# Graph layer on one Trainium2 core: small constant and counting work of the front, moved between VectorE and GpSimd

## The chip, the cores and the metric

The kernel runs on one core of one Trainium2 chip. The metric is the device time of one execution in microseconds. The times before are 1309.93, 1305.32 and 1305.66 us: a median of 1305.66.

The engines are called as the profile calls them: PE (TensorE; PEld is its weight load), DVE (VectorE), ACT (ScalarE), POOL (GpSimd) and SP (SyncE, which only issues DMAs here).

## The reference

```python
h = jnp.maximum(_layernorm(x, axis=-1), 0.0)          # x: 12500 x 128
xs = h[src]                                            # 200000 edges
for i in range(4):                                     # edge types
    mask = (edge_type_4 == i)[:, None]
    msgs = msgs + jnp.where(mask, xs @ W[i] + b[i], 0.0)
return x + jax.ops.segment_sum(msgs, dst, num_segments=12500)
```

The edges are sorted by dst, and dst is drawn as 12500 u², so that the first nodes have very many edges and the last ones few.

## The kernel before, in words

All 200000 edges are taken in chunks of 128. The first C0 = 576 chunks, whose nodes have many edges, are handled densely: for each "slot" (a unit of one to three nodes) PE counts, by a product of two one-hot matrices, how many edges come from each node and of each type, and the counts are then multiplied with the whole table of normalised rows. The other 987 chunks are handled by gathering: GpSimd fetches the 128 rows of a chunk from the table with an indirect DMA, PE sums them by node and type with a one-hot matrix, and DVE adds the results into a ring of sums.

Before this can run at full speed there is the **front**, in which these things go on side by side:

- The table. 33 units of three rows of nodes per partition are loaded from x (`load_span`, on SP's queue). DVE takes statistics (`look`, L519), L523 to L528 make a variance of them, ACT takes the root with `eps` as bias (L531), DVE the reciprocal and the shift (L534, L535), and ACT writes the normalised rows h (L540). PE, ACT and DVE split h into three 16-bit parts (L566 to L582), and SP stores these into htab (L584).
- The rows of x for the first 48 gathered chunks. GpSimd fetches them from x itself (`gather_raw`, L606, 48 indirect DMAs), since the table is not there yet; from the fourth pair on, the gathers are held back behind the statistics of certain units. DVE takes their statistics too, and ACT normalises them (also L540, tile hx).
- The slots (`make_slots`). d1 holds the node that each slot begins with (L926; for further blocks of a node with many edges it is copied by GpSimd, L931). `first_chunk` compares it with the first node of each dense chunk (L937), PE counts the chunks below it (L946), and L950 writes the number qa of the chunk in which the slot's first node lies, for UNITS = 866 units in two pieces of 433. L957 adds each unit's capacity in chunks, `caps`, which gives nth. L961 writes qa of the further blocks, qa of the unit plus the number k of the block, for the slots 866 to 1050. `pick_out` then compares qa and nth with the chunks' numbers (L937 again, the tiles sel), PE picks the edge data with L986, and L994 to L998 put it into `packed`; pieces of 433 come first, then those of the further blocks, in pieces of 185 and below. `unpack` (L1010 on) makes of it what the counting uses.
- Small constants: iotas on GpSimd, their conversions on DVE, memsets.
- `span`, the number of places (nodes) that each gathered chunk may reach: 128 x 8, begun at 10 with a memset and raised in eight steps (L324 to L333), each of a comparison and an addition. It goes into the key of each edge (L362) and into a check of the limits (L370, later L392 and L396).

The order in which each engine meets these instructions is not written by hand in the front: a planner lays it out from the order of the text, the dependencies and its own idea of the costs. It becomes a hand-written order for PE, DVE and ACT only at line 1596 (`manual_schedule`), behind the front. GpSimd's and SP's queues are the planner's throughout. Every engine takes its queue strictly in order. After the front, `pace` distributes the dense work over the groups of gathered chunks.

`eps` is not a plain constant before the change: L489 multiplies an element of srcT (the first transposed source indices) by zero, and L490 adds EPS / UP² to that. So eps, and with it every root, waits for srcT and for two instructions on DVE.

`marks` is a list of instructions of which the last ten hold back some later gathers (L629). The mark of L962 stands at the head of the list, before those of `pick_out` and of `unpack`, of which there are twelve alone; it is not among the last ten.

Of the kernel before, what the change touches and what calls it, by code (L numbers as in the profile page):

```python
# [35 lines left out]
F32 = mybir.dt.float32  # L36
BF16 = mybir.dt.bfloat16
F16 = mybir.dt.float16
# [6 lines left out]
ALU = mybir.AluOpType  # L45
# [5 lines left out]
P = 128  # L51
EPS = 1e-5
# [5 lines left out]
C0 = 576  # L58
# [21 lines left out]
UP = 4096.0  # L80
# [9 lines left out]
def kernel(  # L90
# [10 lines left out]
    nc = tc.nc  # L101
    N, D = x.shape
    E = src.shape[0]
    NT, _, DO = w.shape
# [36 lines left out]
    segs = []  # L141
    for d0, d1, size in ((TWOS, THREES, 2), (HEAVY, ONES, 3), (AFTER, TWOS, 3), (THREES, ND, 3), (ONES, AFTER, 1), (0, HEAVY, 1)):
        segs.append((sum(n for _, n, *_ in segs), (d1 - d0) // size, d0, size, [chunks_of(d, size) for d in range(d0, d1, size)]))
    UNITS = sum(n for _, n, *_ in segs)
    blocks = {}
    NS = 0
    for k, s in (
# [4 lines left out]
        n = sum(c > k for c in segs[s][4])  # L152
# [16 lines left out]
    def window_of(c):  # L169

        m = min((c - C0) // G, FULL)
        end = (C0 + (m + 1) * G if m < FULL else T) * P / E
        a_node = E * ((end**2 + 1 / N) ** 0.5 - end)
        return next((n for n in range(8, WIN, 2) if (n - 1) * a_node > P + 5 * P**0.5), WIN)
# [107 lines left out]
    const = ctx.enter_context(tc.tile_pool(name="const", bufs=1))  # L282
# [6 lines left out]
    srcT = const.tile([P, TURN, P], I32, name="srcT")  # L289
# [31 lines left out]
    row_i = prep.tile([P, BM], I32, name="row_i")  # L321
    nc.gpsimd.iota(row_i, pattern=[[P, BM]], base=0, channel_multiplier=1)
    rowf = const.tile([P, BM], F32, name="rowf")
    nc.vector.tensor_copy(rowf, row_i)  # L324

    span = const.tile([P, BM], F32, name="span")
    more = prep.tile([P, BM], F32, name="more")
    nc.vector.memset(span, float(window_of(C0)))
    for m in range(G, TM, G):
        wider = window_of(C0 + m) - window_of(C0 + m - G)  # L330
        if wider:
            nc.vector.tensor_scalar(more, rowf, m - 0.5, float(wider), ALU.is_gt, ALU.mult)
            nc.vector.tensor_add(span, span, more)  # L333
    QB = max(2, DENSE)

    def prep_edges(m0, m1, prep, QB):
# [148 lines left out]
    nc.vector.memset(ones_b, 1.0)  # L485
    eps = const.tile([P, 1], F32, name="eps")

    zero = const.tile([P, 1], F32, name="zero")
    nc.vector.tensor_single_scalar(zero, srcT[:, 0, 0:1], 0.0, op=ALU.mult)  # L489
    nc.vector.tensor_single_scalar(eps, zero, EPS / UP**2, op=ALU.add)  # L490
    pick = prep.tile([P, NT, N3], BF16, name="pick")
    nc.vector.memset(pick, 0.0)
    for t in range(NT):
# [98 lines left out]
    marks = []  # L592
# [315 lines left out]
    def make_slots(dix):  # L908

        def pieces(a, z, of=512):  # L910
            n = -(-(z - a) // of)
            return [(a + (z - a) * i // n, a + (z - a) * (i + 1) // n) for i in range(n)]

        d1 = dix.tile([P, NS], F16, name="d1")
        qa = dix.tile([P, NS], F16, name="qa")
        nth = dix.tile([P, UNITS], F16, name="nth")
        packed = dix.tile([P, NS], F32, name="packed")
        at_nodes = {}
        for (k, s), (c0, n) in blocks.items():
# [30 lines left out]
            nc.vector.tensor_scalar(qa[:, a:z], pq[:, : z - a], -1.0, 0.0, ALU.add, ALU.max)  # L950

        yield from pipelined(first_chunk(a, z) for a, z in pieces(0, UNITS))
        for u0, n, _, _, caps in segs:
            i = 0
            while i < n:
                m = sum(c == caps[i] for c in caps)
                nc.vector.tensor_single_scalar(nth[:, u0 + i : u0 + i + m], qa[:, u0 + i : u0 + i + m], float(caps[i]), op=ALU.add)  # L957
                i += m
        for (k, s), (c0, n) in blocks.items():
            if k:  # L960
                last = nc.vector.tensor_single_scalar(qa[:, c0 : c0 + n], qa[:, segs[s][0] : segs[s][0] + n], float(k), op=ALU.add)  # L961
        marks.append(last.ins)  # L962
        yield True

        def runs(a, z):
# [98 lines left out]
        for s, (_, n, d0, size, _) in enumerate(segs):  # L1064
            for a, z in pieces(0, n * size):
                pn = x_ps.tile([P, 512], F32, name="pt")
                todo = [(at_nodes[k, r], m * size) for (k, r), (_, m) in blocks.items() if r == s and m * size > a]
                for i, (w0, m) in enumerate(todo):
                    m = min(m, z)
# [337 lines left out]
    building = ExitStack()  # L1407
    dix = building.enter_context(tc.tile_pool(name="dix", bufs=1, side="right"))
    to_slots = make_slots(dix)
    work = None  # L1410
    dense_out = False
# [83 lines left out]
    for gi, us in enumerate(group_of):  # L1495
# [9 lines left out]
        for i, u in enumerate(us):  # L1505
# [7 lines left out]
            last = None  # L1513
            for l in more_looks[:each]:
                last = l()
# [194 lines left out]
    with tc.If(rv > 0):  # L1710
        with tc.tile_pool(name="slow", bufs=1) as slow, tc.tile_pool(name="slow_ps", bufs=1, space=PSUM) as slow_ps:
            zero = slow.tile([P, DO], F32, name="zero")
# [120 lines left out]
```

## Time and profile before

| | |
|---|---|
| median of 3 runs | 1305.66 us |
| lowest, highest | 1305.32, 1309.93 us |
| the profiled execution, its time | 1311.28 us |
| its span, first to last instruction | 1309.6 us |
| busy: PE, DVE, ACT, POOL | 1227.2, 1072.4, 1064.0, 954.0 us |
| mean granted TensorE clock | 0.962 |

Rows of the profile read thus. A row of the timeline has the start and the length in microseconds, the engine, the line of the kernel, the operation, the tile written and the tiles read, the shape, and xN for N instructions merged into one row; in brackets stands the idle time of the engine just before, and who ended it. A row of the groups has the shapes, the count, the busy time in microseconds, the mean duration in nanoseconds, and the idle time before. A row of the windows has the busy time of each engine in a stretch of time. The chain of waits is followed back from the last instruction to whatever released each step.

### The profile page before, as it was taken

The page shows a single profiled execution, that of the slowest core. Times are in us where ns is not written, and L with a number is a line of the kernel's source. Part 1 is how long each engine was busy: PE and PEld are TensorE (multiplying, and loading weights), DVE is VectorE, ACT ScalarE, POOL GpSimd, SP SyncE. Part 2 cuts the span into 40 slices and gives each one's busy share as a digit, 9 for nine tenths or more (in the row PEclk, how much of TensorE's full clock was granted, in tenths as well). Part 3 has the DMA queues.
Part 4 walks back from the last instruction along what each step waited for, and adds up shares of the span by engine and source line. Part 5 has one row for each costly group of instructions (what it writes and reads, how often), then busy time and mean ns, then how long its engine had stood idle before and what let it go on. Part 6 is the DMA issues. An engine that isn't in the chain of part 4 may idle for free.

```text
span 1309.6 us, 30266 instructions
## 1 busy us (share of the span) xinstructions
PE 1227.2 (94%) x9190; PEld 878.9 (67%) x9190; DVE 1072.4 (82%) x5214; ACT 1064.0 (81%) x1814; POOL 954.0 (73%) x1028
## 2 busy tenths in 40 slices
PE   4887898799999999999999999999999999999996
PEld 1345655577777777777777776777777777777775
DVE  8996487897898987989888887879888797978454
ACT  6795644498988989899898988889888898888881
POOL 6727577777777777777777777777777777777772
PEclk9895689799999999999999999999999999999998
DMA  8644289888888888888787877878788788787982
GB/s 252 215 172 145 60 253 335 287 281 254 268 270 253 258 273 259 260 256 275 245 268 243 286 236 254 259 231 276 235 269 250 242 268 252 254 246 242 290 277 83
DMA packets 184229, 321.75 MB, mean 246 GB/s; under 512 B 30100, under 2 KB 82253, under 8 KB 184061
## 3 DMA queue, kind: packets, MB, share of 16 engines
q1 hardware_dynamic: 132701, 214.63, 50.2%
q0 software_dynamic: 46608, 95.52, 25.6%
q10 hardware_dynamic: 4752, 9.64, 1.9%
q8 instruction: 72, 1.18, 0.4%
q14 instruction: 96, 0.79, 0.2%
HBM read 293.99 MB, written 25.67 MB: 244 GB/s over the span
## 4 chain that ended last, share of the span: by engine, by line
PE 81%; ACT 8%; DVE 6%; DMA 2%; issue 2%; SPq 0%; DVEq 0%; ACTq 0%
PE pa L1244 22%; PE pa L1252 22%; PE pt L1138 11%; PE py L701 8%; PE ps L675 7%; ACT dec L1206 2%; PE pt L1297 2%; DMA dtab<-dec 1%; PE pa L1274 1%; DVE ring L764 1%; ACT h L540 1%; PE ps L733 1%; DVE o L1103 1%; PE pt L986 1%; DVE o L1113 1%
## 5 line engine op out<-in xcount | busy, mean ns | idle before, releaser
L622 POOL DMA_INDIRECT hm<-htab,srcT x939 | 900.8, 959 | 311.6 <-issue 194.1
L1206 ACT ACTIVATE dec<-counts 128x1116 fp32r<-128x1116 uint8 (+1 forms) x594 | 676.1, 1162 | 10.2 <-PE pa L1244 7.6
L1103 DVE TENSOR_SCALAR o<-iota_w,hkT 128x392 bf16<-128x392 f16 x1051 | 429.3, 408 | 114.8 <-PE pt L1138 113.3
L1244 PE MATMUL pa<-dec,hs 128*128 128x372 f32 x1764 | 389.9, 355 | 0.0
L1252 PE MATMUL pa<-counts,hs 128*128 128x372 fp8e4 x1764 | 342.5, 327 | 7.8 <-ACT sd L1290 7.8
L1146 ACT CAST counts<-pt 128x396 int32<-128x396 f32 x587 | 292.1, 523 | 39.5 <-PE pt L1138 15.2
L1244 PEld LDWEIGHTS pa<-dec,hs 128*128 128x128 f32 x1764 | 302.3, 188 | 15.6 <-issue 0.3
L1138 PE MATMUL pt<-o,o 128*128 128x396 bf16 x1051 | 280.1, 338 | 12.9 <-DVE o L1113 11.3
L1252 PEld LDWEIGHTS <-hs 128*128 128x128 f16 x1764 | 165.3, 97 | 121.3 <-issue 12.3
L1113 DVE TENSOR_SCALAR o<-iota_b,loT,byT 128x128 bf16<-128x128 bf16 x746 | 245.5, 329 | 0.0
L764 DVE TENSOR_TENSOR ring<-ring,py 128x14 f32 (+6 forms) x912 | 158.4, 174 | 58.0 <-issue 13.0
L665 ACT ACTIVATE sb<-ps 128x224 f32<-128x224 f32 (+7 forms) x235 | 102.6, 437 | 104.7 <-PE py L701 87.5
L675 PEld LDWEIGHTS <-hm 128*128 128x128 f16 x2817 | 142.9, 99 | 66.4 <-issue 13.3
L675 PE MATMUL ps<-oh,hm 128*128 128x56 bf16 (+7 forms) x2817 | 174.0, 198 | 1.6 <-DMA hm<-htab,srcT 1.6
L640 DVE TENSOR_SCALAR oh<-iota_b,keyT 128x56 bf16<-128x56 bf16 (+7 forms) x939 | 161.0, 261 | 6.8 <-PE ps L675 6.8
L701 PE MATMUL py<-sb,wsb 128*128 128x224 f32 (+6 forms) x456 | 122.3, 412 | 0.0
L1138 PEld LDWEIGHTS <-o 128*128 128x128 bf16 x1051 | 82.3, 98 | 55.5 <-DVE o L1113 16.0
L701 PEld LDWEIGHTS py<-sb,wsb 128*128 128x128 f32 x456 | 83.3, 193 | 26.4 <-ACT counts L1146 4.3
L1113 DVE TENSOR_SCALAR o<-iota_b,loT 128x128 bf16<-128x128 bf16 x305 | 83.0, 272 | 0.0
L606 POOL DMA_INDIRECT hx<-in_x_dram,srcT x48 | 46.8, 974 | 22.6 <-issue 9.3
L1274 PE MATMUL pa<-counts,hs 128*128 128x348 fp8e4 x294 | 53.0, 325 | 0.4 <-DMA hs<-htab 0.4
L696 ACT CAST cnt<-pt 128x224 bf16<-128x224 f32 (+10 forms) x61 | 25.7, 421 | 26.1 <-PE pt L692 24.5
(253 smaller groups left out, 789.8 us busy)
## 6 DMA issues: line engine op xcount, KB each, us to landing
hs<-dtab SPq DMA_DIRECT2D x576, 288.0 KB
hm<-htab,srcT POOLq DMA_INDIRECT x939
htab<-h SPq DMA_DIRECT2D x32, 288.0 KB
hs<-htab SPq DMA_DIRECT2D x32, 288.0 KB
dtab<-dec ACTq DMA_DIRECT2D x32, 288.0 KB
xo<-in_x_dram SPq DMA_DIRECT2D x23, 256.0 KB
out_dram<-xo SPq DMA_DIRECT2D x23, 256.0 KB
hm<-in_x_dram SPq DMA_DIRECT2D x18, 192.0 KB
```

The lines of the kernel that those rows point to most:

```text
L622: one = nc.gpsimd.indirect_dma_start(out=hm[:, (i - h0) * D3 : (i - h0 + 1) * D3], out_offset=None, in_=htab, in_offset=bass.IndirectOffse ...
L640: nc.vector.tensor_scalar(oh[:, i, :], iota_b[:, :K], keyf[:, at : at + 1], None, ALU.is_equal)
L675: nc.tensor.matmul(ps[:, i - i0, :], rows(i, c), oh[:, i, :], start=(c == 0), stop=(c == 2))
L701: nc.tensor.matmul(py[:, :g, :], wsb[:, t, :], sb[0][:, :g, t, :], start=False, stop=(t == NT - 1))
L764: nc.vector.tensor_tensor(to, to, of(i), ALU.add)
L1103: one = nc.vector.tensor_scalar(o2[:, k, :NB].rearrange("p (r n) -> p r n", r=ROWS), iota_w, hkT[:, s : s + 1], None, ALU.is_equal)
L1113: one = nc.vector.tensor_scalar(o1[:, k], iota_b, loT[:, s : s + 1], by, ALU.is_equal, ALU.mult)
L1138: one = nc.tensor.matmul(pb, o1, o2, start=first, stop=last)
L1146: lambda i=i, pb=pb: nc.scalar.copy(counts[:, :, i * NT : (i + 1) * NT], pb.rearrange("p (b t) -> p b t", t=NT))
L1206: nc.scalar.activation(decoded[n][:, : j1 - j0, :nv].rearrange("p j (m v) -> p j m v", m=3), by_digit[:, j0:j1, : nu * NT * 4].rearrange(" ...
L1244: nc.tensor.matmul(to.rearrange("p (m v) -> p m v", m=3), row.bitcast(F32R)[:, D // 2 :], decoded[j // DS][:, j % DS, :nv].rearrange("p (m ...
L1252: nc.tensor.matmul(to.rearrange("p (m v) -> p m v", m=3), row[:, :D], counts[:, j, : nu * NT * 4].rearrange("p (v m) -> p m v", m=4)[:, :3 ...
```

## The change

Three places of the front are changed, and nothing behind it.

```diff
     rowf = const.tile([P, BM], F32, name="rowf")
-    nc.vector.tensor_copy(rowf, row_i)
+    nc.gpsimd.tensor_copy(rowf, row_i)
...
-    nc.vector.memset(span, float(window_of(C0)))
+    nc.gpsimd.memset(span, float(window_of(C0)))
     for m in range(G, TM, G):
         wider = window_of(C0 + m) - window_of(C0 + m - G)
         if wider:
-            nc.vector.tensor_scalar(more, rowf, m - 0.5, float(wider), ALU.is_gt, ALU.mult)
-            nc.vector.tensor_add(span, span, more)
+            nc.gpsimd.tensor_scalar(more, rowf, m - 0.5, float(wider), ALU.is_gt, ALU.mult)
+            nc.gpsimd.tensor_tensor(span, span, more, ALU.add)
...
-    zero = const.tile([P, 1], F32, name="zero")
-    nc.vector.tensor_single_scalar(zero, srcT[:, 0, 0:1], 0.0, op=ALU.mult)
-    nc.vector.tensor_single_scalar(eps, zero, EPS / UP**2, op=ALU.add)
+    nc.vector.memset(eps, EPS / UP**2)
...
         nth = dix.tile([P, UNITS], F16, name="nth")
+        room = dix.tile([P, UNITS], F16, name="room")
+        for u0, n, _, _, caps in segs:
+            i = 0
+            while i < n:
+                m = sum(c == caps[i] for c in caps)
+                nc.gpsimd.memset(room[:, u0 + i : u0 + i + m], float(caps[i]))
+                i += m
...
         yield from pipelined(first_chunk(a, z) for a, z in pieces(0, UNITS))
-        for u0, n, _, _, caps in segs:
-            i = 0
-            while i < n:
-                m = sum(c == caps[i] for c in caps)
-                nc.vector.tensor_single_scalar(nth[:, u0 + i : u0 + i + m], qa[:, u0 + i : u0 + i + m], float(caps[i]), op=ALU.add)
-                i += m
+        marks.append(nc.vector.tensor_tensor(nth, qa[:, :UNITS], room, ALU.add).ins)
         for (k, s), (c0, n) in blocks.items():
             if k:
-                last = nc.vector.tensor_single_scalar(qa[:, c0 : c0 + n], qa[:, segs[s][0] : segs[s][0] + n], float(k), op=ALU.add)
-        marks.append(last.ins)
+                nc.gpsimd.tensor_single_scalar(qa[:, c0 : c0 + n], qa[:, segs[s][0] : segs[s][0] + n], float(k), op=ALU.add)
```

Counted out: a conversion and eight pairs of instructions for span go from DVE to GpSimd, with a memset. Two instructions on DVE become one memset for eps, which no longer depends on srcT. Fifteen additions on DVE become one over 866 elements, with the capacities laid down as a row by fifteen memsets on GpSimd. The 27 additions for further blocks (of 1 to 38 elements) go from DVE to GpSimd.

## The prediction

> **What bounds the kernel now.** I read the windows view first, cut where the character of the work changes. Its columns are the stretch, its length, busy microseconds and instruction counts of PE, PEld, DVE, ACT and POOL, then the granted clock, the DMA share and GB/s.
>
> ```profile
> core 0: us, PE busy (x) PEld busy (x) DVE busy (x) ACT busy (x) POOL busy (x), PEclk, DMA share, GB/s
> 8.00:95.00 87.00, 68.16 (x270) 32.20 (x271) 84.76 (x416) 74.57 (x195) 49.45 (x77) 0.96 0.69 221
> 12.00:40.00 28.00, 18.65 (x57) 7.82 (x58) 27.77 (x132) 26.82 (x71) 18.77 (x22) 1.00 0.82 258
> 40.00:55.00 15.00, 13.20 (x42) 5.36 (x41) 13.60 (x82) 10.71 (x27) 12.39 (x37) 0.77 0.70 225
> 55.00:95.00 40.00, 36.31 (x175) 19.02 (x174) 39.40 (x175) 36.96 (x99) 15.20 (x16) 1.00 0.57 196
> 95.00:165.00 70.00, 52.67 (x305) 37.61 (x305) 42.09 (x171) 41.07 (x117) 47.66 (x45) 0.59 0.35 100
> 165.00:1309.60 1144.60, 1105.93 (x8616) 808.90 (x8613) 940.88 (x4583) 946.61 (x1501) 851.46 (x894) 0.98 0.82 257
> ```
>
> From 165 us on, PE is busy 1105.93 of 1144.60 us, and no instruction of the change lies there. The change touches only the first 50 us. There DVE is the full engine: 27.77 of 28.00 us, and 84.76 of 87.00 over the whole front. ACT is next with 74.57 of 87.00. So a microsecond taken from DVE in the front should bring everything behind it one microsecond forward, and nothing in the change can do more than shorten the front.
>
> The chain that ended last, followed back through the front, says where such a microsecond would have to pass (start, length, what):
>
> ```profile
> 29.48 0.48 ACT h L540
> 30.71 3.40 DMA hm<-in_x_dram
> 41.32 0.96 DVE sel L937 x4
> 48.18 1.65 PE pa L569 x2
> 50.46 1.81 PE pt L986 x5
> 58.35 3.12 PE pt L986 x17
> 91.25 5.49 ACT hx L540 x14
> ```
>
> It runs over ACT (the normalised rows, L540), a load of x, DVE's selectors (L937), then PE with the first batches of L986, and at 91.25 reaches the rows of x on ACT. L986 cannot start before the selectors from qa, and these stand in DVE's order behind the very instructions that the change removes.
>
> **The change part by part.** *Limits of places.* L324, L332 and L333 leave DVE: 1 + 8 + 8 instructions, and a memset of eight elements.
>
> ```profile
> L332 DVE TENSOR_SCALAR more<-rowf 128x8 f32<-128x8 f32 x8 | 1.7, 216 | 0.0
> L333 DVE TENSOR_TENSOR span<-span,more 128x8 f32<-128x8 f32 x8 | 1.2, 156 | 0.0
> 9.33 0.15 DVE L324 CAST rowf<-row_i 128x8 f32<-128x8 int32 x1
> 43.21 1.12 DVE L950 TENSOR_SCALAR qa<-pt 128x433 f16<-128x433 f32 x2
> 44.25 0.71 DVE L957 TENSOR_SCALAR nth<-qa 128x287 f16<-128x287 f16 x8
> 46.09 0.86 DVE L957 TENSOR_SCALAR nth<-qa 128x12 f16<-128x12 f16 x7
> 46.87 1.44 DVE L961 TENSOR_SCALAR qa<-qa 128x3 f16<-128x3 f16 x20
> 48.70 0.54 DVE L961 TENSOR_SCALAR qa<-qa 128x8 f16<-128x8 f16 x7
> 49.16 0.81 DVE L937 TENSOR_SCALAR sel<-qa,cidx 128x433 f16<-128x433 f16 x3
> ```
>
> Their durations sum to 1.7 + 1.2 + 0.15 = 3.05 us, but durations on DVE overlap: the merged row at 44.25 shows eight small instructions in 0.71 us, 89 ns from one to the next, and the row at 46.87 twenty in 1.44, 72 ns. With eps's two instructions there are 19. At 89 ns they occupy 1.7 us; the bounds are 1.4 us (72 ns) and 3.5 us (full durations with eps's 0.14 and 0.32). I take 1.7, since these are the same kind of tiny instruction in a full queue.
>
> *The slots' capacities and further blocks.* Fifteen instructions of L957 and 27 of L961 leave: 0.71 + 0.86 + 1.44 + 0.54 = 3.55 us, all on DVE between 44.25 and 49.24. One tensor_tensor over 866 f16 elements comes. The nearest row adds 433 f32 elements:
>
> ```profile
> 64.79 0.58 DVE L998 TENSOR_TENSOR packed<-packed,mask 128x433 f32<-128x433 f32 x1
> ```
>
> At the same rate per element it is at most 2 x 0.58 = 1.16 us; if 16-bit elements go twice as fast, 0.58. I take 0.9, net 3.55 - 0.9 = 2.65 us. DVE loses 1.7 + 2.65 = 4.35 us, less a memset of one element for eps: 4.3 us. With the bounds it is 1.4 + 2.4 = 3.8 to 3.5 + 2.95 = 6.45.
>
> *The root's wait for eps.* Now eps hangs on srcT and stands late in DVE's order.
>
> ```profile
> 8.29 0.15 DVE L528 TENSOR_TENSOR vart<-vart,mvt 128x6 f32<-128x6 f32 x1
> 11.55 0.32 DVE L490 TENSOR_SCALAR eps<-zero 128x1 f32<-128x1 f32 x1
> 11.92 0.30 ACT L531 ACTIVATE rstdt<-vart,eps 128x6 f32<-128x6 f32 x1 [7.80 <-DVE stt L519]
> 12.82 1.26 ACT L540 ACTIVATE h<-hm,nmrt,rstdt 128x128 f32<-128x128 f32 x3 [0.59 <-DVE nmrt L535]
> ```
>
> The row names stt as releaser, but vart is done at 8.44 and eps at 11.87, and the root starts 50 ns later: it is eps. With a memset the root can start about 3.4 us earlier and ACT's first row with it. I do not add this to the 4.3. ACT has a head start then, but the rows behind need DVE's statistics, scales and third parts, and DVE has no idle time between 9.33 and 49.24 to deliver them sooner than its own work allows. Credit: nothing beyond the DVE term, at most what ACT's head start lets DVE use of its idle time (the larger gain below).
>
> *What GpSimd takes on.* A memset, a copy and 16 dependent instructions for the limits, 15 memsets of at most 287 f16 elements, and 27 additions. Its rows:
>
> ```profile
> 37.65 0.15 DVE L926 TENSOR_SCALAR d<-iota_n 128x3 f16<-128x3 f16 x1
> 2.17 0.97 POOL L1439 MEMSET ring<- 128x1056 f32 x1
> 4.40 1.13 POOL L606 DMA_INDIRECT hx<-in_x_dram,srcT  x1 [1.26 <-ACT srcT L355]
> 16.90 0.95 POOL L606 DMA_INDIRECT hx<-in_x_dram,srcT  x1 [3.58 <-DVE stt L519]
> 44.45 3.61 POOL L931 COPY d<-d 128x3 f16<-128x3 f16 x27
> 73.00 0.94 POOL L606 DMA_INDIRECT hx<-in_x_dram,srcT  x1 [4.31 <-DVE varr L525]
> 75.50 0.94 POOL L606 DMA_INDIRECT hx<-in_x_dram,srcT  x1 [0.30 <-issue]
> ```
>
> The 27 copies of L931 have the very shapes of the 27 additions: 3.61 us, 134 ns each. So the additions cost GpSimd 3.6 us. The 17 for the limits are dependent on each other; at 134 to 230 ns (1.7 x L931's pace, for lost overlap) they take 2.3 to 3.9 us, and the memsets of room at most 2.8 us (15 x 134 ns, and 866 elements at the 0.92 ns each of the row at 2.17). In GpSimd's queue stand the 48 gathers of rows of x (L606). Of what comes before the first gather, 1.26 us of idle time swallows a part and the 3.58 us before 16.90 the rest, but for 3.9 + 2.8 - 1.26 - 3.58 = 1.9 us at the upper bounds. The additions make the later gathers 3.6 us late, and the 4.31 us of idle time before 73.00 swallow that, but for 1.2 us at those bounds. The last gather starts at 75.50, and its rows are normalised on ACT only from 91.25 on, so 1.2 us there cost nothing either. I put GpSimd's share at nothing; if this cover were gone, each microsecond of it would stand in front of the row at 91.25.
>
> GpSimd's 134 ns per instruction stand against 1.44 + 0.54 = 1.98 us for the same 27 shapes on DVE, 73 ns each. The Trainium skill ("GPSIMD Engine Reference", section 4.1, Engine selection) says that elementwise work belongs on VectorE, GpSimd being about two times slower for two inputs and near line rate for one; by that rule this move is wrong in total work. The trace agrees on the ratio, 1.8, for one input even, but not on the consequence, as the slower engine is the one that idles here.
>
> **Sum.** The front ends 4.3 us earlier, and everything behind it shifts. The profiled execution took 1311.28 us (span 1309.6); it would take 1307.0. The median of the runs is 1305.66, 5.6 us below the profiled one, and I apply the same difference: 1305.66 - 4.3 = 1301.4 us, 0.33% faster. About 0.5% (6.5 us) is what a measurement of this kernel can tell from no change.
>
> **Rivals.**
>
> *Larger gain, 1297.5.* If ACT's head start of 3.4 us also lets DVE lose its idle time (87.00 - 84.76 = 2.2 us), the gain is 6.5. If besides PE's clock no longer falls to 0.77 between 40 and 55, up to 13.20 x 0.23 = 3.0 us more; half of it makes 8 us. For it: the chain passes over ACT from 12.82 to 29.96. Against: from 48.18 to about 61 the chain lies on PE, whose work is unchanged and which is busy 36.31 of 40.00 us from 55 to 95.
>
> *Nothing arrives, 1305.7.* The front is cut short and the stretch 95 to 165 absorbs it. There no engine is full (PE 52.67 of 70 at clock 0.59). Its first gather of table rows waited 16.53 us for the table:
>
> ```profile
> 92.97 0.94 POOL L622 DMA_INDIRECT hm<-htab,srcT  x1 [16.53 <-ACT hx L540]
> 66.26 0.27 DVE L937 TENSOR_SCALAR sel<-qa,cidx 128x185 f16<-128x185 f16 x1
> ```
>
> That it starts as soon as the table is there speaks for a plain shift and against this case.
>
> *Slower, 1315: the additions stand too far back in GpSimd's queue.* The order of every queue ahead of the hand-written part is made anew by the planner. The additions need qa (43.21 + 1.12 = 44.3); the selectors of the last 185 slots at 66.26 need the additions, and DVE, strictly in order, would stop there. Between 44.3 and 66.26 lie 22 us; less the 3.6 of the additions and at a gather each 0.94 + 0.30 = 1.24 us, 14 gathers may stand ahead of them before DVE waits at all. If they come behind the last gather (75.50 + 1.0 + 3.6 = 80.1), DVE stops 13.8 us: 1305.66 - 4.3 + 13.8 = 1315.2. Against it: L931, whose input was ready at 37.8 (the row of L926), stands at 44.45, 6.6 us and five gathers behind, not thirty-one microseconds.
>
> *GpSimd holds DVE up, 1307.3.* If each of the 44 instructions on GpSimd blocked DVE for its 134 ns, 5.9 us would come back: -4.3 + 5.9 = +1.6. The rows above speak against it: beside L931's copies (44.45 to 48.06) DVE's small instructions came every 72 to 123 ns, after them (48.70) every 77.
> The Trainium skill ("SBUF — State Buffer", section "Who interferes with whom") has such a rule: the two share a pair of ports, and whoever comes second is blocked. By it this case would be the likely one.
>
> **Chances.** Forecast 0.50, larger gain 0.18, nothing arrives 0.15, additions too far back 0.11, GpSimd holds DVE up 0.06. Faster by over 0.5% (below 1299.1) takes the larger gain and the edge of the forecast's bounds (6.45): 0.20. Slower by over 0.5% (above 1312.2) takes the late additions and some 0.03 for other orders of the queues: 0.14. The rest, 0.66, is within 0.5%. The range leaves out the late additions and the far end of the larger gain: 1296.0 to 1309.5.
>
> **What would show it.** Right: DVE's first selector from qa near 45 instead of 49.16, the first row on ACT near 9.4 instead of 12.82, the rows of x on ACT at about 87 instead of 91.25, the first gather of table rows at about 88.7 instead of 92.97, and the stretch behind of the same length. Wrong: idle time of DVE released by GpSimd ahead of L937, gathers of rows of x that end after 80 us, DVE's small instructions that take twice as long beside GpSimd's, or a front that is shorter while the rest is longer by as much.

## The result, and the profile after

The changed kernel takes 1312.72 us (median of 20 runs, 1306.42 to 1317.55); the kernel before, in as many runs, takes 1308.41 us (1303.79 to 1313.07). The ratio is 1.0032 with an interval of 1.0018 to 1.0047: slower by about 4.2 us, where 4.3 us faster was forecast. 1312.72 also lies above the end of the range, 1309.5.

The two profiled executions show only a third of a microsecond between them: 1311.64 us after, 1311.28 before. The profiled one of before lies 2.9 us above its median and that of after 1.1 us below, so 4.0 of the 4.3 us between the medians are missing from the pair. The front is therefore compared place by place, not by the spans.

The first line of the page of after has the busy time, the share of the span and the instructions of each engine:

```profile
PE 1225.6 (94%) x9190; PEld 878.5 (67%) x9190; DVE 1068.2 (82%) x5154; ACT 1064.6 (81%) x1814; POOL 965.3 (74%) x1088
```

DVE has lost 1072.4 - 1068.2 = 4.2 us of work, as forecast (4.3). POOL has gained 965.3 - 954.0 = 11.3 us. The relief as busy time is there; it did not reach the end of the front. The windows of after, with the same cuts as before:

```profile
8.00:95.00 87.00, 65.21 (x252) 29.53 (x253) 74.32 (x327) 69.87 (x179) 62.73 (x132) 0.92 0.66 211
12.00:40.00 28.00, 15.36 (x36) 5.61 (x35) 18.09 (x73) 17.51 (x46) 23.48 (x59) 0.76 0.64 208
40.00:55.00 15.00, 11.53 (x42) 4.45 (x41) 14.76 (x66) 11.46 (x30) 11.32 (x13) 1.00 0.73 229
55.00:95.00 40.00, 36.45 (x174) 18.50 (x173) 37.47 (x165) 37.58 (x99) 26.10 (x60) 1.00 0.64 210
95.00:165.00 70.00, 55.75 (x312) 40.79 (x310) 42.25 (x175) 44.62 (x129) 45.11 (x42) 0.58 0.37 107
165.00:1309.90 1144.90, 1104.20 (x8627) 808.03 (x8627) 946.33 (x4601) 948.30 (x1505) 853.94 (x898) 0.99 0.81 257
```

DVE was busy 27.77 of 28.00 us from 12 to 40; now it is busy 18.09. Some 10 us of the full engine's time are gone, much more than was taken from it. PE and ACT fall with it (18.65 to 15.36, 26.82 to 17.51): from 20 to 24 us neither PE nor DVE nor ACT is busy at all, and GpSimd alone works, for 3.97 of the 4 us. The timeline says who stopped them:

```profile
7.43 0.30 ACT L529 ACTIVATE rstdt<-vart,eps 128x6 f32<-128x6 f32 x1 [5.15 <-DVE vart L526]
8.65 0.88 ACT L538 ACTIVATE h<-hm,nmrt,rstdt 128x128 f32<-128x128 f32 x2 [0.92 <-DVE nmrt L533]
9.43 0.24 ACT L355 CAST srcT<-pt 128x128 int32<-128x128 f32 x1
9.97 1.19 POOL L604 DMA_INDIRECT hx<-in_x_dram,srcT  x1 [5.59 <-ACT srcT L355]
11.20 0.31 POOL L333 TENSOR_TENSOR span<-span,more 128x8 f32<-128x8 f32 x1
11.67 0.96 POOL L604 DMA_INDIRECT hx<-in_x_dram,srcT  x1 [0.16 <-issue]
12.65 0.51 POOL L332 TENSOR_SCALAR more<-rowf 128x8 f32<-128x8 f32 x1
13.34 1.04 POOL L604 DMA_INDIRECT hx<-in_x_dram,srcT  x1 [0.17 <-issue]
...
22.52 0.66 POOL L936 COPY d<-d 128x38 f16<-128x38 f16 x4
23.15 0.24 POOL L332 TENSOR_SCALAR more<-rowf 128x8 f32<-128x8 f32 x1
23.34 1.05 POOL L936 COPY d<-d 128x13 f16<-128x13 f16 x8
24.36 0.19 POOL L333 TENSOR_TENSOR span<-span,more 128x8 f32<-128x8 f32 x1
24.58 0.35 DVE L362 SCALAR_TENSOR_TENSOR sf<-ty,span,si 128x128 f32<-128x128 int32 x1 [8.55 <-POOL span L333]
```

In the kernel before, the last step of the limits and the key that needs them stood almost side by side on DVE:

```profile
14.66 0.15 DVE L333 TENSOR_TENSOR span<-span,more 128x8 f32<-128x8 f32 x1
...
14.93 0.35 DVE L362 SCALAR_TENSOR_TENSOR sf<-ty,span,si 128x128 f32<-128x128 int32 x1
```

Three things are to be read here. Of the sixteen steps of the limits three stand ahead of the first gather, seven each behind a gather, and the last six among room's memsets and the copies of d, so a chain whose own instructions take some 4 us (an estimate, the sum of their sixteen durations) lasts until 24.55. DVE meets the first key (L362), which needs the limits, and stands for 8.55 us; before, the limits were made by 14.81 and the key followed at once. And the root stands ahead of the copy of the source indices (L355) on ACT now, since eps no longer depends on those indices: the copy begins at 9.43 and the first gather at 9.97, where it was 4.40. GpSimd stands idle for 5.59 us ahead of that gather, with thirteen steps of the limits behind it in the queue.

The chain that ended last ran over ACT, a load of x and DVE in the front before. Now it runs over GpSimd:

```profile
9.97 1.19 POOL hx L604
11.67 0.96 POOL hx L604
12.65 0.51 POOL more L332
13.34 1.04 POOL hx L604
...
21.23 0.58 POOL room L920 x10
22.57 0.60 POOL d L936 x4
23.39 0.69 POOL d L936 x6
24.99 0.48 PE pt L367
```

An engine that was off the path has been put on it for 15 us. What that does to the rest of the front (count, then ns of the shortest, median and longest instruction, then first and last start):

```profile
L538 ACT ACTIVATE h<-hm,nmrt,rstdt x98: 477/491/514, 8.6 to 93.9; 128x128 f32<-128x128 f32 x98
L538 ACT ACTIVATE hx<-hx,nmrr,rstdr x48: 477/482/516, 99.5 to 142.4; 128x128 f32<-128x128 f32 x48
L942 DVE TENSOR_SCALAR sel<-qa,cidx x15: 249/321/404, 52.4 to 73.6; 128x433 f16<-128x433 f16 x10, 128x185 f16<-128x185 f16 x5
L1273 PE MATMUL pa<-counts,hs x294: 313/314/496, 169.4 to 243.0; 128*128 128x348 fp8e4 x147
```

The first normalised row is earlier (8.6 for 12.8), as forecast, and the last one later (93.9 for 87.4). Counting the rows of h in the two timelines, the row at a fifth of them is 7.0 us later than before, the middle one 7.7, the last 6.4: the stop at L362 goes through the whole front. The rows of x start at 99.5 for 91.2, the first selector from qa at 52.4 for 49.2, and the dense counting (L1273, before L1274) at 169.4 for 164.5. That last shift, 4.9 us, is near what the medians show.

Whether the stretch behind kept its length, one pair of traces cannot tell. From the start of the dense counting to the end of the span lie 1145.1 us before and 1140.5 after, and in the four partial kernels below 1141.2 to 1143.8; these lengths scatter as widely as the effect is large.

### The profile page after: what moved, and what is told of

It is laid out like the page before. It is cut to its first block, busy times and chain, and to the rows that moved or that the text cites. A ratio compares the mean times of both kernels' runs of the same rounds, so it can differ in the third digit from the quotient of the medians.

```text
span 1309.9 us, 30264 instructions
## 1 busy us (share of the span) xinstructions
PE 1225.6 (94%) x9190; PEld 878.5 (67%) x9190; DVE 1068.2 (82%) x5154; ACT 1064.6 (81%) x1814; POOL 965.3 (74%) x1088
## 4 chain that ended last, share of the span: by engine, by line
PE 79%; DVE 8%; ACT 6%; issue 3%; DMA 2%; POOL 1%; DVEq 1%; SPq 0%; ACTq 0%
PE pa L1243 22%; PE pa L1251 21%; PE pt L1137 11%; PE py L699 8%; PE ps L673 7%; ACT dec L1205 2%; PE pt L1296 2%; DVE ring L762 2%; PE ps L731 1%; DVE o L1102 1%; DVE o L1112 1%; DMA dtab<-dec 1%; PE pt L690 1%; ACT h L538 1%; ACT counts L1145 1%
## 5 line engine op out<-in xcount | busy, mean ns | idle before, releaser
L1137 PE MATMUL pt<-o,o 128*128 128x396 bf16 x1051 | 279.8, 337 | 12.8 <-DVE o L1112 12.1
L663 ACT ACTIVATE sb<-ps 128x224 f32<-128x224 f32 (+7 forms) x235 | 102.7, 437 | 103.1 <-PE py L699 88.8
L1137 PEld LDWEIGHTS <-o 128*128 128x128 bf16 x1051 | 82.2, 98 | 55.2 <-DVE o L1112 16.0
L699 PEld LDWEIGHTS py<-sb,wsb 128*128 128x128 f32 x456 | 84.4, 195 | 26.0 <-ACT counts L1145 3.9
L1112 DVE TENSOR_SCALAR o<-iota_b,loT 128x128 bf16<-128x128 bf16 x305 | 85.9, 282 | 0.0
L1273 PE MATMUL pa<-counts,hs 128*128 128x348 fp8e4 x294 | 51.5, 319 | 0.0
```

The lines of the kernel that those rows point to most:

```text
L699: nc.tensor.matmul(py[:, :g, :], wsb[:, t, :], sb[0][:, :g, t, :], start=False, stop=(t == NT - 1))
L1112: one = nc.vector.tensor_scalar(o1[:, k], iota_b, loT[:, s : s + 1], by, ALU.is_equal, ALU.mult)
L1137: one = nc.tensor.matmul(pb, o1, o2, start=first, stop=last)
```

## The experiments

The theory after the result: the limits, made late in GpSimd's queue, stop DVE; eps makes it worse by moving the gathers between which the limits stand. Its rivals: the additions for further blocks on GpSimd are the loss, or all work on GpSimd is, by making the gathers late.

### One part at a time

Four kernels beside the kernel before (1309.06 us, 35 runs), each with some of the three parts of the change and no other edit.

Only eps:

```diff
-    nc.vector.tensor_single_scalar(zero, srcT[:, 0, 0:1], 0.0, op=ALU.mult)
-    nc.vector.tensor_single_scalar(eps, zero, EPS / UP**2, op=ALU.add)
+    nc.vector.memset(eps, EPS / UP**2)
```

> Only eps becomes a memset; the limits and the slots stay on DVE as before. Theory (the loss is DVE's wait for the limits on GpSimd, which needs both the limits there and the late source indices): ACT takes the source indices about 5 us later, the first gather starts near 10 us instead of 4.4, but DVE waits for nothing on GpSimd, so the time is within 2 us of before, rather below. Rival (the late source indices alone make the loss, by late gathers of rows of x): slower than before by 3 to 5 us, with DVE or ACT waiting for rows of x.

Measured: 1309.26 us, ratio 1.0004 (0.9990 to 1.0019). The first row of h is at 8.9, the first gather at 10.2; the last gather (75.3) and the last row of h (88.0) stand where they stood before (75.5, 87.4). ACT's head start brings no gain that these runs can tell, and gathers that begin 5.8 us late catch up.

Only the limits:

```diff
-            nc.vector.tensor_scalar(more, rowf, m - 0.5, float(wider), ALU.is_gt, ALU.mult)
-            nc.vector.tensor_add(span, span, more)
+            nc.gpsimd.tensor_scalar(more, rowf, m - 0.5, float(wider), ALU.is_gt, ALU.mult)
+            nc.gpsimd.tensor_tensor(span, span, more, ALU.add)
```

> Only the limits (rowf, span, more) go to GpSimd; eps still depends on the source indices. Theory: the chain stands between gathers, but the gathers start at 4.4 us, so the limits end near 18 us instead of 24.6 and DVE waits for them by 2 to 4 us; less the 1.7 us that leave DVE, the time is 0 to 3 us above before. Rival (late source indices alone): no slower than before, 1 to 2 us faster.

Measured: 1312.24 us, ratio 1.0018 (1.0005 to 1.0032). The timeline has the stop, shorter since the gathers begin at 4.4 here:

```profile
17.98 0.35 DVE L362 SCALAR_TENSOR_TENSOR sf<-ty,span,si 128x128 f32<-128x128 int32 x1 [2.07 <-POOL span L333]
```

Eighteen instructions have left DVE, and yet the row of h at a fifth is 2.3 us late and the last one 4.2 us (91.6). Of the parts alone it is the only one that is measurably slower. But the wait is not its whole price: relief and wait give -1.7 + 2.07 = +0.4 us, and the interval of the ratio stands for 0.7 to 4.2 us. What the rest is, no run shows.

Only the slots (room, one tensor_tensor, the 27 additions on GpSimd):

```diff
-                nc.vector.tensor_single_scalar(nth[...], qa[...], float(caps[i]), op=ALU.add)
+        marks.append(nc.vector.tensor_tensor(nth, qa[:, :UNITS], room, ALU.add).ins)
...
-                last = nc.vector.tensor_single_scalar(qa[:, c0 : c0 + n], ..., float(k), op=ALU.add)
+                nc.gpsimd.tensor_single_scalar(qa[:, c0 : c0 + n], ..., float(k), op=ALU.add)
```

> Only the slots' part: capacities as a row, additions for further blocks on GpSimd. Theory: 2.5 to 3 us faster than before, as DVE loses 3.55 us of small instructions and gets one of 0.6. Rival (the additions on GpSimd, 8.2 us for 27 in the changed kernel, hold up the gathers or DVE and make part of the loss): not faster, or slower by up to 3 us, with DVE waiting for qa from GpSimd.

Measured: 1309.70 us, ratio 1.0007 (0.9992 to 1.0022). DVE waits 2.8 us for the additions at the selectors of the further blocks, and the last gather comes at 82.2 for 75.5. The theory had forecast 2.5 to 3 us less and missed; the rival had forecast this.

Eps and the slots, that is, all but the limits:

> The whole change without the limits, which stay on DVE. Theory: 2.5 to 4 us faster than before, since the wait for the limits (8.55 us in the changed kernel) is gone and the rest stays. Rival (late source indices alone): still slower than before by 1 to 4 us.

Measured: 1308.60 us, ratio 0.9994 (0.9979 to 1.0010). The groups view, with the idle time before the group and its releaser at the end of the row:

```profile
L961 POOL TENSOR_SCALAR qa<-qa 128x1 f16<-128x1 f16 (+8 forms) x27 | 6.7, 256 | 1.3
L942 DVE TENSOR_SCALAR sel<-qa,cidx 128x433 f16<-128x433 f16 (+1 forms) x15 | 4.7, 341 | 4.7 <-POOL qa L961 4.7
```

DVE waits 4.7 us for the additions here, the last gather starts at 84.4 and the last row of h at 92.6, and the kernel is still no slower. It is no faster either, where the theory had forecast 2.5 to 4 us. The changed kernel differs from this one by the limits alone, and the intervals of the two ratios, 1.0018 to 1.0047 and 0.9979 to 1.0010, lie apart: without the limits on GpSimd the change costs nothing that these runs can tell.

In these five changed kernels the start of the dense counting goes with the time, to within 1 us. Against the kernel before it comes 4.9 us later in the whole change, 4.2 with the limits alone, 1.5 with the slots, and 0.4 and 0.6 earlier with eps and with eps and slots; the medians moved by +4.3, +3.2, +0.6, +0.2 and -0.5. The end of the rows of h does not go with the times: with eps and slots it is 5.2 us late at no cost. In that kernel the row at a fifth is 0.8 us early and the middle one 0.8 late, where the whole change has 7.0 and 7.7: its rows fall behind only near the end.

The granted clock of PE between 8 and 95 us is lower in the two slower kernels (0.92 in the whole change, 0.90 with the limits alone) than in the kernel before and in the other three (0.95 to 0.96). Whether the lower clock only follows from the stop or is a part of the loss, no run separates.

### Orders and single costs, on other chips

The fourteen runs that follow fell on two other chips, on which the kernel before itself takes 1574.67 to 1598.01 us, so their ratios are compared among themselves and not with those above. Their traces show further waits in the front, some of them for nothing that the trace names, so one trace of each says less here.

Capacities as one row, with the additions left on DVE:

```diff
-                nc.vector.tensor_single_scalar(nth[...], qa[...], float(caps[i]), op=ALU.add)
+        nc.vector.tensor_tensor(nth, qa[:, :UNITS], room, ALU.add)
```

> Only the capacities as one row (15 additions on DVE become one tensor_tensor over 866 elements, the row laid down by GpSimd); the 27 additions for further blocks stay on DVE. Theory (the slots' gain was eaten by GpSimd's slow additions, 8 us instead of 3.6, which held up DVE and the gathers of rows of x): no wait for qa, the last gather of rows of x at about 76 us as before, and 0.5 to 1.5 us faster than before. Rival (no microsecond taken from DVE in the front reaches the end): within 0.5 us of before, with the first gather of table rows not earlier than 92.5.

Measured: 1575.41 against 1574.67 us, ratio 1.0003 (0.9976 to 1.0030): no gain to be seen, but the 0.5 to 1.5 us forecast lie within this interval.

Eps by memset, with the copy of the source indices kept ahead of the first root. The order is one of the queue alone, with no semaphore ("source first" below):

```diff
+        src_copied.append(nc.scalar.copy(srcT[...], pg[:, :n, :]).ins)
...
+            one = nc.scalar.activation(rstd[:, :n], var[:, :n], AF.Sqrt, bias=eps, ...)
+            if src_copied:
+                tc.add_manual_dep(one.ins, src_copied.pop().name, ...)
```

> eps as a memset, with an order on ACT that keeps the copy of the source indices ahead of the first root. Theory: the first gather is back at about 4.4 us and the first row on ACT still near 9; as DVE is full, the time is that of eps alone, within 1.5 us of before. Rival (the late source indices cost what the early root gains): 2 to 4 us faster than before.

Measured: 1576.89 us, ratio 1.0005 (0.9980 to 1.0030). The first gather is at 4.4 again and the first row of h at 11.7; nothing is won that these runs can tell.

The whole change with source first:

> The whole change with the copy of the source indices kept ahead of the first root on ACT. Theory (the wait for the limits is made long by the late source indices, since the chain stands between the gathers): first gather at 4.4 us, limits done at 18 to 19, DVE's wait for them 1 to 4 us instead of 8.55, and the time 2 to 4 us below the changed kernel, so 0 to 2 us above before. Rival (the place of the source indices does not matter, the chain is long by itself): wait still above 6 us and the time that of the changed kernel, 4 us above before.

Measured: 1580.06 us, ratio 1.0055 (1.0033 to 1.0076). The first gather starts at 4.6 and the wait at the key falls to 4.0 us, as forecast; the time, forecast at 0 to 2 us above before, does not follow. (The profiled execution, 1571.99 us, is the fastest of the twelve, so its trace need not show the loss.)

The slots with copies in place of the additions, and the numbers k added by one instruction on DVE:

```diff
-                nc.gpsimd.tensor_single_scalar(qa[:, c0 : c0 + n], ..., float(k), op=ALU.add)
+                nc.gpsimd.tensor_copy(qa[:, c0 : c0 + n], ...)
+        nc.vector.tensor_tensor(qa[:, UNITS:], qa[:, UNITS:], kth, ALU.add)
```

> The slots' part alone, with GpSimd's 27 additions replaced by 27 copies of the same shapes in the same place of its queue, and one tensor_tensor on DVE over the 185 elements that adds the block numbers from a row. Theory: the copies take 3.6 to 4.5 us instead of 8, DVE's wait of 2.8 us for qa goes, the last gather of rows of x comes near 79 instead of 82, and the time is 1 to 2.5 us below that of the slots' part alone (ratio about 0.999 to before). Rival (their length does not matter): the time of the slots' part alone, ratio 1.0007.

Measured: 1583.81 us, ratio 1.0045 (1.0025 to 1.0064).

```profile
L967 POOL COPY qa<-qa 128x1 f16<-128x1 f16 (+8 forms) x27 | 3.4, 183 | 0.0
L968 DVE TENSOR_TENSOR qa<-qa,kth 128x185 f16<-128x185 f16 x1 | 0.3, 259 | 4.6 <-POOL qa L967 4.6
```

A copy costs 183 ns where the addition of the same shapes cost 256, but DVE waits 4.6 us all the same: the theory, 1 to 2.5 us below the slots' part, missed. That cheaper instructions came with no shorter wait speaks for the place in the queue, more than the price of one, as what sets it; it does not show it, since the chip is another one and the reader is one instruction over all 185 elements.

The whole change, with the second gather ordered behind the last addition of the limits ("limits ahead"):

```diff
+            span_made = [nc.gpsimd.tensor_tensor(span, span, more, ALU.add).ins]
...
+            if span_made:
+                tc.add_manual_dep(one.ins, span_made.pop().name, ...)
```

> The whole change, with one order added: the second gather of rows of x comes behind the last addition of the limits in GpSimd's queue, with no wait between them; nothing of the work changes. Theory (the changed kernel is slower because the sixteen steps of the limits stand one by one between the gathers, so that VectorE stood 8.55 us at the keys): the limits end near 14 us instead of 24.4, VectorE's wait at L362 falls from 8.55 us to under 1, and the kernel loses the 4 us again: ratio 0.998 to 1.000 against the kernel before. Rival (any work of GpSimd's in the first 25 us delays the gathers, and the delayed rows of x set the front's end): the wait is gone but the gathers start later, and the ratio stays at 1.002 to 1.004.

Measured: 1587.83 against 1575.28 us, ratio 1.0069 (1.0040 to 1.0097). The limits end at 17.2 and the wait is 3.5 us. The theory forecast an end near 14, a wait under 1 us and 0.998 to 1.000, and missed all three: the first gather, which waits for the source indices until 10.2, still stands ahead of most of the limits.

Both orders together:

> As the run before, and the copy of the source indices kept ahead of the first root on ScalarE, so that the first gather starts near 4.4 us again instead of 10. Theory (two orders of the planner are the whole loss): limits done by about 14 us, no wait at L362, last gather of rows of x near 81 us instead of 86.5, ratio 0.996 to 0.999. Rival (the slots' additions on GpSimd eat the rest): VectorE waits 2 to 5 us for qa at the selectors of the further blocks, and the ratio is 0.999 to 1.001.

Measured: 1581.47 us, ratio 1.0031 (1.0005 to 1.0057). The key comes at 13.8 after a wait of 0.6 us, and the kernel is slower than before still; the theory, 0.996 to 0.999, missed. In the middle of this front stands a row that no expectation had:

```profile
50.22 0.19 DVE L523 TENSOR_TENSOR mvt<-stt 128x30 f32<-128x30 f32 x1 [6.10 <-remote]
```

The trace names no engine and no transfer of this kernel as the releaser of those 6.10 us.

Only the limits, with limits ahead:

> Only the limits on GpSimd (eps and slots as before the change), with the same order: the second gather of rows of x behind the last addition of the limits. Theory (the wait and the interleaving are the price of the limits, 2 to 4 us): the wait of 2.1 us at L362 goes, the ratio falls from 1.0018 to 0.998 to 1.000. Rival (the sixteen steps cost the gathers their own 3 to 5 us wherever they stand, and that is the price): ratio 1.001 to 1.003 still.

Measured: 1575.60 us, ratio 1.0001 (0.9980 to 1.0023). No wait at the key, and no loss that these runs can tell; the end of the theory's range, 1.000, fits. No gain either, with 18 instructions off DVE.

Eps with source first, and the capacities as one row:

> Of the change only what takes work away or does it in fewer instructions: eps by memset, with the copy of the source indices kept ahead of the first root, and the capacities added as one row (the 27 additions for further blocks and the limits stay on VectorE). VectorE loses 2 small instructions and 15 additions less one of 0.6 us: about 0.2 + 1.57 - 0.6 = 1.2 us. Theory (VectorE's relief does arrive if no wait takes its place): ratio 0.998 to 0.9995, hardly apart from none. Rival (relief in the front never arrives, the rows of x set its end): 1.000 to 1.001.

Measured: 1575.84 us, ratio 0.9999 (0.9976 to 1.0022): no gain that these runs can tell.

### The parts by twos, beside the whole

The kernel before took 1598.01 us in these runs. The whole change again:

> The whole change once more, beside the runs that follow, as their yardstick. All theories: 1.002 to 1.005, VectorE 7 to 9 us at L362 behind the limits.

Measured: 1609.73 us, ratio 1.0073 (1.0049 to 1.0096).

Eps and limits, without the slots:

> Eps and limits as in the change, the slots as before. Theory A (the wait for the limits is the loss; eps makes it longer, since it moves the gathers and with them the limits between them about 5 us back): VectorE waits 4 to 7 us at L362 and the ratio is that of the whole change, 1.002 to 1.005. Theory B (the slots' additions on GpSimd, with the wait for qa and the late gathers, are the loss): no slower than before, 0.999 to 1.001.

Measured: 1607.53 us, ratio 1.0057 (1.0035 to 1.0079).

Limits and slots, without eps:

> Limits and slots as in the change, eps as before. Theory A: the copy of the source indices comes before the roots again, the limits end 4 to 5 us earlier than in the whole change, VectorE waits 2 to 4 us at L362 instead of 8.55, and the ratio is 1.000 to 1.002. Theory B: as the whole change, 1.002 to 1.005, with VectorE waiting for qa ahead of the selectors of the further blocks.

Measured: 1599.75 us, ratio 1.0003 (0.9986 to 1.0020).

The whole with limits ahead, as in the earlier run:

> The whole change with the second gather of rows of x ordered behind the last addition of the limits in GpSimd's queue. Theory A: the wait at L362 falls from over 7 us to under 4, ratio 0.999 to 1.001. Theory B: the wait goes and the ratio stays at that of the whole change or rises, 1.002 to 1.006, since the gathers and the additions behind them come later still.

Measured: 1611.16 us, ratio 1.0084 (1.0057 to 1.0111).

The waits of DVE for the limits (us in total, times, longest), of the whole, of eps and limits, of limits and slots, and of the whole with limits ahead:

```profile
DVE sf L362 <- POOL span L333: 8.8, 1, 8.8
```

```profile
DVE sf L362 <- POOL span L333: 7.5, 1, 7.5
```

```profile
DVE sf L362 <- POOL span L333: 2.2, 1, 2.2
```

```profile
DVE sf L362 <- POOL span L333: 3.5, 1, 3.5
```

The first three settle which parts it takes: limits and eps without the slots are about as slow as the whole, limits and slots without eps are not slow. The slots as the main cause of the whole's loss have fallen, on this chip too. In these three the length of the wait goes with the time, 8.8 and 7.5 against 2.2: eps adds over 5 us to the wait, and the slots about one. The fourth row speaks against the wait as the only price: 5 us less of it and no time won. The same four kernels by their rows of h, in the same order:

```profile
L538 ACT ACTIVATE h<-hm,nmrt,rstdt x98: 478/492/519, 8.9 to 112.9; 128x128 f32<-128x128 f32 x98
```

```profile
L538 ACT ACTIVATE h<-hm,nmrt,rstdt x98: 479/494/537, 8.7 to 111.7; 128x128 f32<-128x128 f32 x98
```

```profile
L540 ACT ACTIVATE h<-hm,nmrt,rstdt x98: 477/486/512, 11.3 to 101.0; 128x128 f32<-128x128 f32 x98
```

```profile
L538 ACT ACTIVATE h<-hm,nmrt,rstdt x98: 477/487/517, 9.0 to 113.5; 128x128 f32<-128x128 f32 x98
```

The last row of the table tells slow from not slow: 112.9, 111.7 and 113.5 against 101.0. With limits ahead the last row of h is as late as in the whole change, though the key came earlier.

### Both orders, without one or the other

Everything but the additions, with both orders:

> Everything of the change but the 27 additions (they stay on VectorE), with both orders added: the copy of the source indices ahead of the first root, and the second gather of rows of x behind the last addition of the limits. Theory A (what the change loses is waits behind GpSimd's queue; without the wait for the limits and without the one for qa VectorE's relief is left): no wait of VectorE over 1 us for GpSimd, last gather of rows of x within 3 us of the kernel before's, ratio 0.997 to 0.9995. Theory B (GpSimd's late gathers alone make the front late, whoever waits): the limits hold the second gather until about 13 us, the last gather is 3 to 6 us late, ratio 1.001 to 1.004.

Measured: 1582.81 against 1576.12 us, ratio 1.0033 (1.0013 to 1.0053). DVE waits 0.6 us for the limits; the last gather is at 95.7, the last row of h at 107.5.

Everything but the limits, with source first:

> Everything of the change but the limits (they stay on VectorE), with the copy of the source indices kept ahead of the first root. Theory A: no wait at L362; VectorE waits 2 to 5 us for the additions' qa at the selectors of the further blocks; what that costs and VectorE's relief of 2.65 us cancel, ratio 0.999 to 1.001. Theory B: the additions make the last gathers 5 to 9 us late, ratio 1.002 to 1.005.

Measured: 1580.09 us, ratio 1.0017 (1.0000 to 1.0035), at the edge of what can be told. The last gather is at 89.6, the last row of h at 103.1.

Neither theory holds cleanly for these two: with hardly a wait left (0.6 us), limits and eps with the capacities as one row still lose 0.3% on this chip. Over the fourteen runs on the two other chips, the five kernels of ratio 1.0005 or less end the rows of h between 99.8 and 105.0; 1.0017 belongs to 103.1, and the eight of 1.0031 and above to 107.5 to 113.5. The dense counting parts them too: it starts between 185.5 and 190.5 in the five, at 186.0 in the one of 1.0017, and between 191.0 and 201.3 in the eight. So on these chips a late table and a late start of the counting are what the slower kernels have in common. That is a relation and not a cause: eps and slots, on the chip of the first four experiments, had the late end of the table without the loss. And the row of 6.10 us above shows that these fronts hold stops that the trace puts down to nothing in the kernel.

## Why the prediction was wrong, step by step

**What failed: "I put GpSimd's share at nothing".** The prediction weighed what GpSimd took on as occupied time, against idle time in GpSimd's queue ("Of what comes before the first gather, 1.26 us of idle time swallows a part and the 3.58 us before 16.90 the rest"). For the limits that was the wrong quantity. Their result has a reader on the full engine, the key at L362, and what counts is when the last of sixteen dependent steps ends. On DVE they stood among other small work and were done by 14.81. In GpSimd's queue three were done before the first gather, seven each stood behind a gather of 0.96 to 1.19 us, the last six among the memsets of room and the copies of d, and they were done at 24.55. DVE stopped 8.55 us, and PE and ACT with it. Put into the prediction's own sum it gives -4.3 + 8.55 = 4.25 us, and the medians differ by 4.3. That the two agree so well is partly luck: the same sum gives 0.4 us for the limits alone, where the medians differ by 3.2, and no run shows DVE's relief arriving.

The prediction did have this mechanism, as the rival "the additions stand too far back in GpSimd's queue", and gave it 0.11. It priced it for the additions, whose reader comes 22 us later, and not for the limits, whose reader came within a microsecond of their last step. The question was the right one and was asked of the wrong instructions.

**Eps, credited with nothing: right in the gain, and blind to the cost.** The first row on ACT came at 8.65 (near 9.4 was forecast) and brought no gain that eps alone could tell (1.0004, 0.9990 to 1.0019). What was missed is that a dependency taken away lets the planner change an order: the root overtook the copy of the source indices, and the first gather came 5.57 us later, with the steps of the limits that stand behind it. Alone, that is free. With the limits in the same queue the wait is 8.55 us (7.5 without the slots, on another chip) where without eps it is about 2. That eps costs by this order is not shown: with the order put back and the wait at 4.0 us the kernel was still slower (1.0055).

**DVE's relief of 4.3 us: right in size, not shown to arrive.** 4.2 us of busy time are gone. The one tensor_tensor took 0.59 us, at the lower bound of 0.58 to 1.16. But the step that "a microsecond taken from DVE in the front should bring everything behind it one microsecond forward" was borne out by no run. The kernels that take work from DVE without a wait for GpSimd (1.0003, 1.0005, 1.0001, 0.9999) are no faster that these runs can tell; the 0.3 to 2 us that they take away, an estimate by the terms of the prediction, is too little for that. Rows from the timeline of after, later in the front:

```profile
53.69 0.59 DVE L958 TENSOR_TENSOR nth<-qa,room 128x866 f16<-128x866 f16 x1
...
68.46 0.59 DVE L997 TENSOR_TENSOR packed<-packed,mask 128x433 f32<-128x433 f32 x1
68.62 0.54 POOL L961 TENSOR_SCALAR qa<-qa 128x13 f16<-128x13 f16 x1
...
71.23 0.48 DVE L942 TENSOR_SCALAR sel<-qa,cidx 128x185 f16<-128x185 f16 x2 [0.61 <-POOL qa L961]
```

**The additions at 134 ns: mis-sized.** The price was taken from L931, copies of the same shapes. GpSimd's rows of the same timeline, copies first:

```profile
55.76 2.29 POOL L936 COPY d<-d 128x3 f16<-128x3 f16 x15
...
62.99 8.20 POOL L961 TENSOR_SCALAR qa<-qa 128x38 f16<-128x38 f16 x27
```

8.20 us for 27 are 304 ns each, 4.6 us more than the forecast 3.6. In the changed kernel that cost DVE only 0.61 us (the row at 71.23), where everything ahead of it was late already. Where the limits stayed on DVE, it was 2.8 us of waiting with the slots alone and 4.7 with eps and slots. That the slots' gain went there is argued and not shown, since the capacities as one row, with the additions left on DVE, brought no visible gain either.

**"GpSimd holds DVE up": against it, as argued.** DVE's addition of two tiles in SBUF at 68.46 lies inside the 8.20 us of GpSimd's additions and takes 0.59 us; in the kernel before, beside gathers, it took 0.58 (the row at 64.79). The rule of the Trainium skill ("SBUF — State Buffer", section "Who interferes with whom") is narrower than the prediction has it: it is for DVE instructions with two operands in SBUF, or in a mode that takes both ports, and whoever issues first holds the other up. By it DVE can hold up GpSimd as well, and this trace agrees with that side. GpSimd's addition at 68.62, of 13 elements, took 537 ns beside DVE's, which had begun first. Of its 23 additions of at most 13 elements nineteen took 210 to 243 ns; the other four, 297 to 537 ns, each lay beside that instruction or beside a selector (L942). That the ports are the reason no run shows. The other page of the Trainium skill that the prediction cites ("GPSIMD Engine Reference", section 4.1) has GpSimd near line rate for one input. For these instructions, of 1 to 38 elements, the 304 ns against the 73 ns of the same 27 additions on DVE are four times as much, and the measurement decides.

**The shift behind the front: right in kind, as far as it can be seen.** The start of the dense counting moved with the medians, to within 1 us, in the whole change (4.9 us) and its four parts; that the stretch behind keeps its length the traces can neither show nor deny. The sign was wrong because the front got longer.

**What stays open.** That the limits on GpSimd make the change slower is shown by leaving them out (0.9994 for 1.0032). That on another chip the limits with eps lose, and the limits with the slots do not, is shown by the parts by twos (1.0057 and 1.0003). That the wait at the key is all of their price is argued from the trace of the changed kernel and from the sum, and the limits alone speak against it (0.4 us by the sum, 3.2 measured). With the wait shortened by an order the kernel stayed slower than before (1.0055, 1.0069, 1.0084), and with 0.6 us of it left 1.0031 and 1.0033 remained. Those runs were on chips whose fronts have further stops; the orders were not tried on the chip of the first four experiments, and no run put all of the limits ahead of the first gather. No version was found that beats the kernel before.

## What to carry to other kernels

That an engine has idle time does not make work moved to it free: look up who reads the result, when that reader comes, and behind what each dependent step will stand in the new queue; a chain of small steps that stands between transfers ends with the transfers, however short its own steps are (4 us of work took until 24.55). Taking away a dependency is an edit to the order of the queues too, where a planner makes the order: read the order that comes out before pricing the rest. Take the price of an instruction from a row with the same operation, not only the same shapes.

## What the runs showed of the hardware

GpSimd took 304 ns from one 16-bit tensor_scalar of 128 x 1 to 128 x 38 to the next (8.20 us for 27), 153 ns for copies of the same kind of shapes (2.29 us for 15), and 190 to 310 ns for a tensor_tensor of 128 x 8, all in the changed kernel.

The kernel before took 1308 us on one chip and 1575 to 1598 us on two others, where the dense stretch moved 207 GB/s (limits and slots, from 165 us on) instead of 257. One of these two gave 1574.67, 1598.01 and 1576.12 us in three sets of runs.
